# Two cross-attentions on one core: layer-0 values as eight one-head matmuls on 64×32 parts of the array

## The chip, the cores and the metric

The kernel runs on one core of a Trainium2 chip. The metric is device time in microseconds (us), from start to end of one execution; lower is better. A core has a matmul engine (PE, with its weight loads shown apart as PEld), a vector engine (DVE), a scalar engine (ACT), GpSimd (POOL) and a queue engine (SP) that issues most DMAs here. They run side by side and wait for each other by semaphores.

## The reference

Two cross-attention layers follow each other on x, which is 4 batches × 1024 rows × 1024 columns in fp32, with a context of 64 rows a batch. What matters here is the attention of layer 0:

```
q = x Wq + bq;  k = ctx Wk + bk;  v = ctx Wv + bv
# 32 query heads of 32 columns; 8 key/value heads, each shared by 4 query heads
attn = softmax(q k^T / sqrt(32) + mask)      # 64 keys for each row and head
out  = attn v                                # for each head: 64 keys -> 32 columns
x1   = layernorm(out Wo + bo + x)
```

Layer 1 is a second attention with 16 heads of 64 columns and a gated residual. All is computed in fp32.

## The kernel before, in words

The rows of x are worked in 32 tiles of 128 rows (NSUB), eight tiles to a block, two tiles to a pair. The time falls into four stages:

1. Keys and values of both layers are computed from the context (lines 312 to 359). K0 and V0 are kept in one SBUF tile `kv0`, both block-diagonal over two heads: `v0bd` holds, for each batch, head group c and half i, a 128 × 64 matrix whose rows are two heads' 64 keys and whose columns are these heads' 32 columns each, with zeros off the diagonal. `nc.gpsimd.memset(kv0, 0.0)` writes the zeros (line 307) and eight small DMAs the values (line 343).
2. Queries. `query_steps` computes a block's queries by a seven-product scheme (Strassen's, in Winograd's form) on PE (line 551), ACT and DVE add (lines 562, 568), and SP writes them to DRAM as `qTd` (line 565).
3. Attention of layer 0, by `mix(t, count)` for each tile t. The stage interleaves a tile's attention with other work: for tiles 0 to 23 the query steps of the next blocks, for tiles 24 to 31 `folded_queries` (line 832 and 838), which folds layer-1 weights.
4. Output projection of layer 0 (`project`, line 415, with `folded_values`, line 859, among its first pairs), then layer 1. This is some 1215 us and is not touched by the change, but for the form in which it is given Wo.

Within stage 3 a tile goes through these steps. `load_queries` brings q from qTd and the mask (lines 622, 626). `front(c)` makes the scores of half the heads with eight matmuls on 64 rows of the array each (line 655), in pairs that lie on rows 0 to 63 and 64 to 127; DVE adds the mask (line 659), takes the largest (666) and subtracts (669), ACT takes the exponential (673, 681), DVE sums, inverts and divides (686, 687, 690). Then the probabilities have to be turned, keys to partitions: for tiles 0 to 18 (`by_turning`) through DRAM (POOL issues, lines 703 and 707) and two DVE transposes of 32×32 blocks, which the text calls flips (line 391), for tiles 19 to 31 by PE (line 382) and an ACT copy (line 386). Each tile has two turned halves, `pTs[0]` and `pTs[1]`, one for each c.

`values()` then multiplies (line 722). Each of its four matmuls takes 128 rows (two heads' keys) and 64 columns (the same two heads) of the array and 512 moving columns (four query heads × 128 rows of the tile):

```
for c in range(2):
    bank = ps[:, c * 512 : (c + 1) * 512] if by_turning(t) else ps[c]
    for i in range(2):
        nc.tensor.matmul(bank[i * 64 : (i + 1) * 64], v0bd[:, b, c, i, :],
            pTs[c][:, i * 4 : (i + 1) * 4].rearrange("p g l -> p (g l)"), ...)
```

The result lies in two PSUM banks, `big` for tiles 0 to 18 and two `wx` for the others. ACT copies it out (`copy_out`, lines 373 and 375) and writes it to DRAM as `oTd` (line 728), from where the projection loads it. Each fp32 matmul of the program appears in the profile as two weight loads and two matmul records.

A planner, not the order of the source, sets the order of instructions on each engine: it places them by costs that it assumes and by what must be ready. So an edit in one place can move instructions in others. Each engine carries out its own list in order.

Wo comes to `right_weight(wo0, "wa", "wo0")` (line 910) in a row order that the host has set; `block_of` loads each of its four blocks with one DMA of 1 MB (line 148). The buffers of tag `wa` that it goes to are those of the layer-0 query weights, so its loads wait until PE has used these for the last time.

Of the kernel before, what the change touches and what calls it, by code (L numbers as in the profile page):

```python
# [8 lines left out]
F32 = mybir.dt.float32  # L9
# [5 lines left out]
P = 128  # L15
# [4 lines left out]
B = 4  # L20
L = 1024
S = 64
# [7 lines left out]
Q = 32  # L30
NQ = P // Q
QW = H // NQ
PPB = NPAIR // B
HEADS0 = 32
BY_HEAD = 16

# [32 lines left out]
def tile_two_cross_attentions(  # L71
# [25 lines left out]
    nc = tc.nc  # L97

    def sub_ap(t):
        return slice(t * P, (t + 1) * P)  # L100
# [9 lines left out]
    def big():  # L110
        return ps_big.tile([P, 1024], F32, tag="big", name="big")

    def one():
        return big()[:, 0:512]

    def wx():
        return ps_wx.tile([P, 512], F32, tag="wx", name="wx")
# [17 lines left out]
    def new_block(tag, name):  # L135
        return wpool.tile([P, HK, HW], F32, tag=tag, name=name)

    def block_of(w, i, j, tag, name, turned=False):
        t = new_block(tag, name)
        cols = slice(j * HW, (j + 1) * HW)  # L140
        if turned:
            rows = w.rearrange("(a k j) o -> a j k o", a=NQ, j=Q)
            for a in range(NQ):
                nc.sync.dma_start(
                    out=t[a * Q : (a + 1) * Q], in_=rows[a, :, i * HK : (i + 1) * HK, cols]
                )
        else:
            nc.sync.dma_start(
                out=t, in_=w[i * HW : (i + 1) * HW, cols].rearrange("(k p) o -> p k o", p=P)
            )  # L150
        return t
# [28 lines left out]
    def right_weight(w, tag, name, turned=False):  # L180

        r = {"B11": block_of(w, 0, 0, tag, f"{name}_B11", turned)}
        r["T1"] = block_of(w, 0, 1, tag, f"{name}_B12", turned)
        r["B22"] = block_of(w, 1, 1, tag, f"{name}_B22", turned)
        r["B21"] = block_of(w, 1, 0, tag, f"{name}_B21", turned)
        for n in ("T3", "T2", "N4"):
            r[n] = new_block(tag, f"{name}_{n}")
        return r, right_sums(r)
# [7 lines left out]
    kv0pool = open_pool(attention, "kv0", 1, "right")  # L196
# [8 lines left out]
    for i in range(2):  # L205
        t = scratch.tile([P, H], F32, tag="cnat", name=f"ctx_{i}", bufs=2)
# [3 lines left out]
    for w, n in ((wk0, "wk0"), (wv0, "wv0")):  # L210
        t = wpool.tile([P, KC, 256], F32, tag="wb", name=n)
# [91 lines left out]
                )  # L303
        return ct

    kv0 = kv0pool.tile([P, 2048], F32, tag="kv0", name="kv0")
    nc.gpsimd.memset(kv0, 0.0)

    k0bd = kv0[:, 0:1024].rearrange("p (b c n) -> p b c n", b=B, c=2)
    v0bd = kv0[:, 1024:2048].rearrange("p (b c i n) -> p b c i n", b=B, c=2, i=2)  # L310

    ct = transpose_ctx(0)
    for c in range(2):
        ps = one()
# [13 lines left out]
    for bb in range(2):  # L328
        ps = one()
        for k in range(KC):  # L330
            nc.tensor.matmul(
                ps[:, 0:256], ct[:, k, sub_ap(bb)], wkv0[1][:, k, :],
                start=(k == 0), stop=(k == KC - 1),
# [4 lines left out]
    for e in range(2):  # L338
        for i in range(2):
            j = 2 * i + e  # L340
            for c in range(2):
                at = c * P + j * 32
                nc.sync.dma_start(
                    out=v0bd[e * S : (e + 1) * S, :, c, i, e * 32 : (e + 1) * 32],
                    in_=v0d[:, at : at + 32].rearrange("(b s) d -> s b d", b=B),
                )
    ct = transpose_ctx(1)
    kv1 = []
    for w, dst, n in ((w1k, kTd, "k1"), (w1v, vTd, "v1")):
        kvT = kv1pool.tile([P, KC, B * S], F32, tag="k1", name=n)  # L350
        for c in range(KC):
            ps = one() if c % 2 else wx()
            for k in range(KC):
                nc.tensor.matmul(  # L354
                    ps[:, 0:256], w[k // HK, c // HK][:, k % HK, sub_ap(c % HK)], ct[:, k, :],
                    start=(k == 0), stop=(k == KC - 1),
# [256 lines left out]
    def by_turning(t):  # L613


        return t < NSUB - SUB - 5
# [12 lines left out]
    def attend0(t):  # L629
# [12 lines left out]

        n = BY_HEAD if by_turning(t) else 0

# [51 lines left out]
    def outputs0(t):  # L696

        b = t * P // L
        s = probs.pop(t)
        pTs = {}  # L700
        if by_turning(t):

            nc.gpsimd.dma_start(out=p0[t], in_=s)
            pq = pqpool.tile([P, NQ, 512], F32, tag="pq", name=f"pq0_{t}")
            v = p0[t].rearrange("(u i) (a w) -> a i u w", i=Q, a=NQ)
            for a in range(NQ):
                nc.gpsimd.dma_start(out=pq[a * Q : (a + 1) * Q], in_=v[a])

        def flip(c):
            pT = pTs[c] = ppool.tile([P, 8, P], F32, tag="pT", name=f"pT0_{t}_{c}")  # L710
            if by_turning(t):
                turn_quarters(pq, pT, (c * 8, (c + 1) * 8))
                return
            turn(s[:, c * 1024 : (c + 1) * 1024], pT)

        def values():
            oT = opool.tile([P, KC, P], F32, tag="oT", name=f"oT0_{t}")
            ps = big() if by_turning(t) else [wx(), wx()]
            for c in range(2):
                bank = ps[:, c * 512 : (c + 1) * 512] if by_turning(t) else ps[c]  # L720
                for i in range(2):
                    nc.tensor.matmul(  # L722
                        bank[i * 64 : (i + 1) * 64], v0bd[:, b, c, i, :],
                        pTs[c][:, i * 4 : (i + 1) * 4].rearrange("p g l -> p (g l)"),
                        start=True, stop=True,
                    )
            copy_out(oT.rearrange("p g l -> p (g l)"), ps)
            nc.scalar.dma_start(out=oTd[t // 2][:, :, sub_ap(t % 2)], in_=oT)

        return flip, values  # L730

    turned = {}
# [60 lines left out]
    rows, fills = rows0(0)  # L793
# [5 lines left out]
    rows, fills = rows0(1)  # L799
# [88 lines left out]
    def other_work(rows):  # L888

        nonlocal fold, early, bo_sb, w_o, first_outputs  # L890
        for blk in range(1, NBLK):
            steps = query_steps(blk, rows)
            fills = {}
            if blk + 1 < NBLK:
                rows, fills = rows0(blk + 1)
            for n, step in enumerate(steps):
                step()
                if n in fills:
                    fills[n]()
                if n == len(steps) - 1:  # L900
                    load_queries(blk * SUB)
                yield
        queries_cm.close()
        fold = open_pool(fold_cm, "fold", 1)

        early = open_pool(early_cm, "early", 1)
        kT = fold.tile([P, KC, B * S], F32, tag="kvT", name="kT")
        nc.sync.dma_start(out=kT, in_=kTd)
        wch = chunk(wq1, 0, "wq1")
        w_o, w_o_sums = right_weight(wo0, "wa", "wo0")  # L910
        bo_sb = constant(bo0.partition_broadcast(P), [P, H], "bo", F32, fold)
        for k in range(KC):
            ahead = chunk(wq1, k + 1, "wq1") if k + 1 < KC else None
            for step in folded_queries(kT, wch, k):
                step()
                yield
            wch = ahead
            if k == 3:
                run(w_o_sums)
            if k == 5:  # L920
                first_outputs = load_outputs(0)
# [10 lines left out]
    n = 28 * (NBLK - 1) - AHEAD  # L932
# [5 lines left out]
    n = 5 * KC - 2 * AHEAD  # L938
# [59 lines left out]
    for pair in range(NPAIR):  # L998
        r, a = ahead_r, ahead_a
# [29 lines left out]
        if pair == NPAIR - 2:  # L1029
            xq = load_x1(0)  # L1030
            turned = turn_x1(0, xq, o2pool, "o2")
# [79 lines left out]
    for pair in range(NPAIR):  # L1111
# [10 lines left out]
        if (pair + 2) % PPB == 0 and pair + 2 < NPAIR:  # L1122
            b = (pair + 2) // PPB
# [3 lines left out]
        if (pair + 1) % PPB == 0 and pair + 1 < NPAIR:  # L1127
            b = (pair + 1) // PPB
# [68 lines left out]
```

## Time and profile before

| | |
|---|---|
| runs, device time | 1946.58, 1947.51, 1951.64 us; median 1947.51 |
| profiled execution | 1952.53 us, of which the span of its instructions is 1950.5 |
| PE busy, granted clock | 1895.1 us (97%), 0.99 |
| DVE, ACT, POOL busy | 1272.0, 385.2, 289.6 us |
| line 655, matmuls of the scores | 1024 records, 85.7 us |
| line 722, matmuls of the values | 152 records into big, 38.6 us; 104 into wx, 26.1 us |
| flips, pT<-pq, line 391, up to tile 18 | 38, 44.9 us, 1219 ns each |
| stage 3 | from about 194 to 735 us of the span |

A matmul record's own duration holds its way through the array; records overlap, so busy time is the union of them and not their sum. "x8" counts records. `128*64` is the part of the array in use, rows × columns. In the chain of waits a piece lasts until the next piece begins, so there a burst is given by the time that it holds up PE. Windows are stretches of the span; a gap on an engine matters only where the chain passes through it. The median of the runs is 5.0 us below the profiled execution.

### The profile page before, as it was taken

Reading aid. Unit: us, or ns where it says so; the run is one execution under the profiler, and the core shown is the slowest. Engines: PE = TensorE matmul, PEld = TensorE weight load, DVE = VectorE, ACT = ScalarE, POOL = GpSimd, SP = SyncE. Lnnn points to the kernel's source line nnn. Section 1 sums busy time; section 2 is a strip of 40 time slices with the busy share of each in tenths; the row PEclk is TensorE's granted clock in tenths of the full one; section 3 lists DMA queues with packets and bytes.
Section 4 is the critical chain, followed back from the end, with each engine's and each line's share of the span. In section 5 each row is a group of like instructions: output and inputs, shape, how many; then the busy total and the mean of one; then the engine's idle time right before and its main releaser. Section 6 shows DMA issues by size and latency. Waiting matters only on the chain.

```text
span 1950.5 us, 16583 instructions
## 1 busy us (share of the span) xinstructions
PE 1895.1 (97%) x5904; PEld 896.4 (46%) x5904; DVE 1272.0 (65%) x1540; ACT 385.2 (20%) x1028; POOL 289.6 (15%) x198
## 2 busy tenths in 40 slices
PE   8999998998998989999999999999999999999999
PEld 7744444443445654334343444444444444444444
DVE  3424798887878984355367667557665766576653
ACT  1111553643535761221200001000000000000000
POOL 0000111111100104445546542000000000000000
PEclk9999999998999999999999999999999999999999
DMA  8971689796775985666572325374747474747421
GB/s 275 183 190 65 177 237 261 223 254 214 231 214 187 302 258 186 193 217 215 178 231 98 142 83 151 108 172 130 183 119 181 121 183 120 182 125 178 119 87 43
DMA packets 217986, 342.07 MB, mean 175 GB/s; under 512 B 25264, under 2 KB 140336, under 8 KB 212912
## 3 DMA queue, kind: packets, MB, share of 16 engines
q1 hardware_dynamic: 156544, 255.03, 46.4%
q10 hardware_dynamic: 52544, 46.14, 8.6%
q0 software_dynamic: 8816, 39.85, 7.1%
q8 instruction: 46, 0.75, 0.2%
q14 instruction: 36, 0.29, 0.1%
HBM read 203.34 MB, written 137.63 MB: 175 GB/s over the span
## 4 chain that ended last, share of the span: by engine, by line
PE 84%; DVE 9%; DMA 3%; ACT 2%; issue 1%; SPq 0%; DVEq 0%; ACTq 0%
PE wx L415 59%; PE wx L551 14%; PE big L655 3%; DVE s L659 2%; DVE mx L666 2%; PE big L859 1%; PE wx L354 1%; PE big L354 1%; DMA q<-qTd 1%; PE big L722 1%; DVE s L669 1%; DMA qTd<-z 1%; ACT s L673 1%; PE wx L832 1%; DVE sm L686 1%
## 5 line engine op out<-in xcount | busy, mean ns | idle before, releaser
L423 DVE TENSOR_TENSOR r<-wx,r 128x512 f32<-128x512 f32 x224 | 153.5, 686 | 269.0 <-PE wx L415 266.6
L477 ACT ACTIVATE s<-s 128x1024 f32<-128x1024 f32 x32 | 33.7, 1056 | 651.8 <-DVE s L476 642.8
L427 DVE TENSOR_TENSOR s<-wx,key_bias 128x512 f32<-128x512 f32 x64 | 44.1, 689 | 137.3 <-PE wx L415 134.5
L551 PE MATMUL wx<-xT,wq_S 128*128 128x512 f32 x256 | 119.3, 602 | 1.6 <-ACT z L562 1.6
L884 POOL TENSOR_TENSOR r<-r,bo 128x1024 f32<-128x1024 f32 x32 | 79.2, 2482 | 263.1 <-DMA r<-in_x_dram 254.6
L415 PE MATMUL wx<-wo_B,S 128*128 128x512 f32 x256 | 116.8, 599 | 1.4 <-DVE r L423 1.4
L415 PE MATMUL wx<-b_B,pT 128*128 128x512 f32 x256 | 115.8, 593 | 0.6 <-ACT pT L386 0.6
L415 PE MATMUL wx<-b_B,S_p 128*128 128x512 f32 x256 | 116.0, 596 | 0.0
L551 PE MATMUL wx<-xB,wq_A 128*128 128x512 f32 x256 | 115.5, 596 | 0.0
L415 PE MATMUL wx<-a_B,xT 128*128 128x512 f32 x256 | 115.4, 592 | 0.0
L415 PE MATMUL wx<-a_B,S_x 128*128 128x512 f32 x256 | 115.3, 593 | 0.0
L673 ACT ACTIVATE s<-s,mx 128x64 f32<-128x64 f32 x304 | 101.1, 334 | 70.8 <-DVE mx L666 64.6
L415 PE MATMUL wx<-wo_B,o 128*128 128x512 f32 x256 | 113.5, 596 | 0.0
L659 DVE TENSOR_TENSOR s<-big,m 128x1024 f32<-128x1024 f32 x64 | 77.0, 1217 | 46.6 <-PE big L655 46.5
L655 PE MATMUL big<-kv,q 64*128 64x128 f32 x1024 | 85.7, 298 | 15.0 <-DMA q<-qTd 14.9
L655 PEld LDWEIGHTS big<-kv,q 64*128 64x128 f32 x1024 | 73.2, 200 | 51.2 <-issue 45.2
L966 POOL TENSOR_TENSOR r<-r,gamma 128x1024 f32<-128x1024 f32 x32 | 76.0, 2376 | 137.1 <-DVE r L284 137.1
L967 POOL TENSOR_TENSOR r<-r,beta 128x1024 f32<-128x1024 f32 x32 | 80.4, 2513 | 2.4
L415 PEld LDWEIGHTS wx<-wo_B,S 128*128 128x128 f32 x256 | 47.3, 190 | 67.1 <-issue 53.6
L391 DVE STREAM_TRANSPOSE pT<-pq 128x1024 f32<-128x1024 f32 x66 | 77.9, 1218 | 0.0
L690 DVE TENSOR_TENSOR s<-s,sm 128x1024 f32<-128x1024 f32 x64 | 77.2, 1222 | 1.0
L415 PEld LDWEIGHTS wx<-wo_B,o 128*128 128x128 f32 x256 | 48.0, 190 | 63.5 <-issue 63.0
(159 smaller groups left out, 2993.6 us busy)
## 6 DMA issues: line engine op xcount, KB each, us to landing
p<-s POOLq DMA_DIRECT2D x19, 1024.0 KB, 8.3
pq<-p POOLq DMA_DIRECT2D x76, 256.0 KB, 6.2
xq<-in_x_dram SPq DMA_DIRECT2D x64, 256.0 KB, 10.2
q<-qTd SPq DMA_DIRECT2D x32, 512.0 KB, 8.3
oTd<-oT ACTq DMA_DIRECT2D x32, 512.0 KB, 7.4
ad<-a SPq DMA_DIRECT2D x16, 1024.0 KB, 7.3
o<-oTd SPq DMA_DIRECT2D x16, 1024.0 KB, 8.8
r<-in_x_dram SPq DMA_DIRECT2D x32, 512.0 KB, 4.1
```

The lines of the kernel that those rows point to most:

```text
L391: nc.vector.transpose(dst.rearrange("p k (u i) -> p k u i", i=Q), t[:, :, k0 * Q : k1 * Q].rearrange("p u (k j) -> p k u j", j=Q),)
L415: nc.tensor.matmul(bank, a[s][:, k, :], w[m][:, k, :], start=first and k == 0, stop=last and k == HK - 1, skip_group_check=True,)
L423: nc.vector.tensor_tensor(at, bank, at, ALU.add)
L427: nc.vector.tensor_tensor(at, bank.rearrange("p (h s) -> p h s", s=S), bias.unsqueeze(1).to_broadcast([P, 512 // S, S]), ALU.add,)
L551: nc.tensor.matmul(bank, w_q[a][:, k, sub_ap(i)], rows[b][:, k, :], start=first and k == 0, stop=last and k == HK - 1, skip_group_check=True,)
L655: nc.tensor.matmul(ps[:, at : at + P], q[on, c * 4 + g, :], k0bd[on, b, c, :], start=True, stop=True,)
L659: nc.vector.tensor_tensor(quarters[:, :, c * 8 : (c + 1) * 8], ps.rearrange("p (k a l) -> p a k l", a=NQ, l=Q), mask.rearrange("p e (h l) ...
L673: nc.scalar.activation(heads[:, 0, k], heads[:, 0, k], AF.Exp, bias=mx[:, 0, k : k + 1], accum_out=sm[:, 0, k : k + 1],)
L690: nc.vector.tensor_tensor(heads[:, e], heads[:, e], wide(sm[:, e]), ALU.mult)
L884: nc.gpsimd.tensor_tensor(ru, ru, bo_sb, ALU.add)
L966: nc.gpsimd.tensor_tensor(r[u], r[u], gamma0_sb, ALU.mult)
L967: nc.gpsimd.tensor_tensor(r[u], r[u], beta0_sb, ALU.add)
```

## The change

V0 is kept as it is, without zeros: `v0` holds for each batch, c and i the 64 keys × 32 columns of one head on partitions 0 to 63 (e = 0) and of another on 64 to 127 (e = 1). `values()` makes eight matmuls instead of four. Each has one head's 64 keys on one row half of the array (rows e·64) and 32 of its columns (columns (2c + i)·32), with 512 moving columns as before. The eight parts cover the array once. The bank is now chosen by e, not by c, so the two row halves write to different banks.

With that the rows of `oT` lie in another order, and Wo has to match: `block_of` gets a third form, `"heads"`, which loads each of the four blocks with four DMAs of 32 partitions (256 KB each). `kv0` becomes a quarter smaller, and the memset covers the keys' half alone.

```diff
-        if turned:
+        if turned == "heads":
+            rows = w.rearrange("(c g i e d) o -> c i e d g o", c=2, g=4, i=2, e=2)
+            for a in range(NQ):
+                nc.sync.dma_start(
+                    out=t[a * Q : (a + 1) * Q], in_=rows[a // 2, a % 2, i][:, :, cols]
+                )
+        elif turned:
...
-    kv0 = kv0pool.tile([P, 2048], F32, tag="kv0", name="kv0")
-    nc.gpsimd.memset(kv0, 0.0)
+    kv0 = kv0pool.tile([P, 1536], F32, tag="kv0", name="kv0")
+    nc.gpsimd.memset(kv0[:, 0:1024], 0.0)
...
-    v0bd = kv0[:, 1024:2048].rearrange("p (b c i n) -> p b c i n", b=B, c=2, i=2)
+    v0 = kv0[:, 1024:1536].rearrange("p (b c i d) -> p b c i d", b=B, c=2, i=2)
...
-                    out=v0bd[e * S : (e + 1) * S, :, c, i, e * 32 : (e + 1) * 32],
+                    out=v0[e * S : (e + 1) * S, :, c, i, :],
...
             for c in range(2):
-                bank = ps[:, c * 512 : (c + 1) * 512] if by_turning(t) else ps[c]
                 for i in range(2):
-                    nc.tensor.matmul(
-                        bank[i * 64 : (i + 1) * 64], v0bd[:, b, c, i, :],
-                        pTs[c][:, i * 4 : (i + 1) * 4].rearrange("p g l -> p (g l)"),
-                        start=True, stop=True,
-                    )
+                    for e in range(2):
+                        bank = ps[:, e * 512 : (e + 1) * 512] if by_turning(t) else ps[e]
+                        on, at = slice(e * S, (e + 1) * S), (2 * c + i) * 32
+                        nc.tensor.matmul(
+                            bank[at : at + 32], v0[on, b, c, i, :],
+                            pTs[c][on, i * 4 : (i + 1) * 4].rearrange("p g l -> p (g l)"),
+                            start=True, stop=True, tile_position=(e * S, at),
+                        )
...
-        w_o, w_o_sums = right_weight(wo0, "wa", "wo0")
+        w_o, w_o_sums = right_weight(wo0, "wa", "wo0", "heads")
```

## The prediction

> **What bounds the kernel now.** I read first the sums by engine, to see who is nearly full; then the windows, cut where the chain of waits changes hands, because the change lives in one stage; then the chain and the order of time inside them, for what a shorter burst is worth there.
>
> ```profile
> PE 1895.1 (97%) x5904; PEld 896.4 (46%) x5904; DVE 1272.0 (65%) x1540; ACT 385.2 (20%) x1028; POOL 289.6 (15%) x198
> ```
>
> ```profile
> 194.00:244.00 50.00, 50.00 (x216) 23.75 (x216) 36.69 (x38) 25.43 (x108) 6.21 (x11) 1.00 0.62 174
> 244.00:334.00 90.00, 83.76 (x326) 37.15 (x326) 80.52 (x79) 42.52 (x180) 13.69 (x25) 0.99 0.91 242
> 334.00:411.00 77.00, 76.95 (x320) 37.08 (x318) 67.06 (x69) 41.49 (x178) 11.06 (x21) 0.97 0.82 239
> 411.00:480.00 69.00, 61.34 (x232) 26.93 (x230) 54.22 (x52) 28.18 (x111) 10.86 (x20) 0.97 0.83 243
> 480.00:567.00 87.00, 85.99 (x366) 41.11 (x366) 70.15 (x70) 38.24 (x123) 10.41 (x19) 0.97 0.73 215
> 567.00:735.00 168.00, 150.66 (x1019) 98.84 (x1016) 144.35 (x145) 102.11 (x154) 6.15 (x3) 0.95 0.79 247
> ```
>
> The columns are length, then busy time of PE, PEld, DVE, ACT and POOL, clock and DMA. The reader is to see two kinds of stretch. In 194–244, 334–411 and 480–567 PE has hardly a gap, and the chain of waits is all PE. In the other three PE has 6, 8 and 17 us of gaps, DVE is 89, 79 and 86% busy, and the chain runs along DVE and, twice, through the write and reload of qTd. All values matmuls (line 722) lie in these six. Two bursts on the chain, one whole and one that the built order has split, and from the timeline one burst that waits and the flips it waits for:
>
> ```profile
> 376.52 1.87 PE big L722 x8
> 378.39 1.09 PE big L655 x16
> ...
> 393.74 1.02 PE big L722 x4
> 394.76 0.42 PE big L655 x2
> 395.17 1.01 PE big L722 x4
> ```
>
> ```profile
> 319.79 2.12 PE L722 MATMUL big<-pT,kv 128*64 128x512 f32 x8 [0.65 <-DVE pT L391]
> ```
>
> ```profile
> 318.40 2.36 DVE L391 STREAM_TRANSPOSE pT<-pq 128x1024 f32<-128x1024 f32 x2
> ```
>
> Each program matmul is two records. A whole burst (8 records, four matmuls) holds PE 1.87 us. The records of the trace show why: they start in pairs, 0.006 us apart, at 0, 0.48, 0.91 and 1.34 us; so the two 64-column halves already stream together, and a pair takes 0.43 us as a full-width record does. 4 × 0.43 = 1.72, and 0.15 for change of layout and a first weight load. The last two lines show the other limit: the two flips of one tile end 1.13 us apart, and the burst began right after the first.
>
> **What the Trainium skill says.** "TensorE: Matmul & The Clock Gate", Part 3: matmuls on different row and column strips run at once, starting about 4 ns apart; sixteen tiles of 32×32 at 512 columns came out 10.6 times faster. The trace agrees for two column halves (above) and for two row halves (line 655: pairs 0.007 us apart, sixteen records in 1.09 us); eight parts it does not show. "TensorEngine Tiling (Array Packing)", Restrictions and Gotchas: row tiles must not share a PSUM bank at one time, which the change respects by giving each row half a bank. The first page, Part 1, on the clock gate: an idle window of about 3.4 us halves the clock. Here half-clock windows last 3.4, 6.8 or 10.2 us and stand behind PE's longest gaps (at 329, 473, 614 us).
>
> **The change part by part.**
>
> *Burst alone.* Eight matmuls, each on its own 64×32 part: all first passes side by side, then all second passes. 0.48 + 0.43 + 0.09 for the exit = 1.00 us (the split half above, two matmuls on two parts, takes just that: 1.01), plus 6 × 0.007 = 0.04 for the further starts. I take 1.02 against 1.87: 0.85 us, times 32 = 27 us at most.
>
> *What holds it back: the second flip.* The four matmuls of c = 1 need the second pT. Before, its lateness hid behind the 0.86 us of c = 0. Now all want to start together, and a second flip that is d late costs d. Set the end of each flip against the first start of its burst, in the records: in 8 of the 32 tiles d is 0.89 to 1.0 us (PE was waiting for the first flip, and the second comes 1.13 later), in 5 more, all turned on PE, 0.86 to 2.2; in the rest −1.07 to 0.58. A burst with d near 1 costs 1.03 + 1.01 = 2.04 whether it has four matmuls or eight: saved, nothing.
>
> *What stands on the path.* Saving = 1.87 − (1.02 + max(0, d + 0.05)), bursts on the chain only. Tile 0 (d 0.20): 0.6. 334–411: tile 6 (d −0.08) 0.85; tile 7 (0.89) 0; tile 8 (0.43) 0.4; tile 9 (0.98), split, 2.45 with 0.11 of score work inside becomes 2.04: 0.3; half of tile 10: 0.15; sum 1.7. 480–567: tile 14 (−0.67) 0.85, tile 15 (0.45) 0.35, tiles 16 and 17 (0.23) 0.57 each, tile 18, split, 0.5; sum 2.8. 567–735: tile 26 0.7, tile 23 (0.86) 0. The last tile: before, c = 1 stands behind a matmul of line 859 that waits for vT (landed at 727); in the built order after, all eight come first and four matmuls of line 415 stand ahead of line 859. Values end at 724.66 + 1.17 + 1.01 = 726.8 instead of 729.2, less 0.5 for the line-859 pair now done later: 1.8. Total 7.6 us.
>
> *Order.* The built order moves: it split 10 bursts before and splits 2 after; values of tiles 9 to 21 stand two to six matmuls earlier, and DVE's flips with them, often ahead of a division. Each such place is worth up to a few us to either side; I take 0 and keep ±4 for the range.
>
> *Wo.* Its four loads become sixteen, with 2 KB pieces as before. Twelve more issues on SP at about 0.4 us (0.38 to 0.43 in the trace) are 5 us of SP's time around 520–570, in front of q and mask loads. Those go out a tile (about 15 us) ahead, and Wo is first used for its sums near 598: hidden. Without that cover: up to 5 us late for a score matmul; kept in the ±4. Queueing behind a busy weight buffer is no new wait (SP waits on PE for line 148 14.2 us in three places already).
>
> *Nothing.* The memset halves, 1.81 to about 0.9 us on POOL; behind it the identity is ready at 3.0, and PE waits for ctx until 4.64. The eight V0 loads keep number and size. copy_out reads as many columns.
>
> **Sum.** The profiled execution took 1952.53, span 1950.5 and 2.0 around it; 7.6 off gives 1944.9. The median of the runs is 5.0 lower, so 1947.5 − 7.6 = 1939.9.
>
> **The rivals.**
>
> 1. *The gain is swallowed* (0.25). DVE is 87% busy in 334–411; once PE arrives earlier it waits for the first flip in more tiles, each then has d near 1, and the qTd reload (9.8 us at 470) takes the rest; one more half-clock window of 6.8 us costs 3.4. Against it: tiles 14 to 17 had their first flip 0.7 to 1.8 us before PE came. Gain −4 to 5: 1942 to 1951.
>
> 2. *The full stretches are not the only ones* (0.15). In 244–334 PE is 93% busy as well, and DVE waits for score matmuls 46.5 us in all (20 times). If DVE gets its scores earlier everywhere, the other tiles' 0.4 to 0.86 count too: all 32 by the formula give some 14, and with merged bursts 15 to 22: 1926 to 1932.
>
> 3. *Slower: four column parts over the same 64 rows don't stream together* (0.08). Place: the burst. If only a row pair runs at once, eight matmuls take 4 × 0.86 + 0.15 = 3.6 us, 1.7 more than now; on some 15 bursts of the chain +26, on all 32 +55: 1973 to 2002. It decides at four wide: then a burst takes 1.87 and nothing is lost. The two-wide overlap both ways speaks against it.
>
> 4. *The change doesn't do what it says*: parts run four wide, burst unchanged at 1.87; inside rival 1's numbers.
>
> **How the numbers follow.** 0.3% is 5.8 us, about what a measurement of this kernel can tell from no change. The likeliest case (0.52) spans gains of 3 to 14, and most of it lies over 5.8: 0.43 faster, 0.09 same. Rival 1: 0.19 same, 0.05 slower, little faster. Rival 2 is faster, rival 3 slower. Together 0.59 faster, 0.28 same, 0.13 slower. The likeliest case alone would span 1933 to 1945. For 8 in 10 I reach to 1928, which takes most of rival 2, and to 1951, which takes rival 1; rival 3 stays out.
>
> **What would show it right or wrong.** Right: a values burst of 16 records with eight starts within 0.06 us and 1.0 us on the chain where the flips are early, about 2.0 where they are not; matmul time of the line (38.6 and 26.1 us now, in its two groups) down by 14 to 27 us, while PE's gaps before it that DVE or ACT ends (7.1 and 6.3 us now) grow; line 415's first matmul some 2 us earlier after the last tile; the stretch after 735 unchanged at about 1215. Wrong: bursts of 1.9 or 3.6 us (the overlap), a span that falls by 15 or more (slack on DVE was larger than I read), or a longer wait at q or mask loads near 560–620 (SP).

## The result, and the profile after

The changed kernel takes 1946.39 us (median of 12 runs) beside 1949.38 for the kernel before on the same chip: ratio 0.9979, 95% interval 0.9968 to 0.9989, or some 4 us less. (The ratio is the one on record; the two medians themselves lie 3.0 us apart.) The forecast was 7.6 us less. A burst costs what the prediction's formula says, but most of the 4 us comes with the new order of instructions, and by the profiles more than half of that at the last tile. The shorter bursts themselves bring about 1 us, which can't be told from nothing, where the sum had 5.8 for them and for the joining of split ones.

| | before | after |
|---|---|---|
| profiled execution, span | 1952.53, 1950.5 | 1946.74, 1944.5 |
| values matmuls busy, two groups | 38.6 + 26.1 | 33.9 + 19.9 |
| first matmul of the projection to the end | 1221.3 | 1221.8 |
| half-clock time, mean of the runs | 34 to 37 (five sets of runs) | 45 |

Half-clock time is the time that the granted clock of PE stood at half, worked out as 2 × (1 − mean granted clock) × span. Lines move down in the new file: the scores are line 662, the values 733, the flips 398, the projection 422, the subtraction of the largest 676, the fold of the layer-1 weights 843.

The sums by engine and the windows, columns as before:

```profile
PE 1885.5 (97%) x6160; PEld 892.9 (46%) x6160; DVE 1276.9 (66%) x1540; ACT 384.7 (20%) x1028; POOL 288.4 (15%) x198
```

```profile
194.00:244.00 50.00, 50.00 (x234) 24.43 (x234) 36.98 (x39) 25.84 (x108) 6.21 (x11) 1.00 0.61 179
244.00:334.00 90.00, 85.48 (x387) 38.10 (x386) 84.00 (x83) 42.74 (x181) 13.69 (x25) 0.98 0.92 258
334.00:411.00 77.00, 76.17 (x369) 34.59 (x368) 69.01 (x71) 42.61 (x183) 13.66 (x25) 1.00 0.83 234
411.00:480.00 69.00, 63.44 (x285) 29.22 (x283) 57.78 (x56) 33.01 (x140) 10.40 (x19) 0.98 0.82 245
480.00:567.00 87.00, 85.32 (x428) 39.46 (x428) 69.87 (x76) 36.38 (x96) 8.23 (x15) 1.00 0.81 221
567.00:735.00 168.00, 144.08 (x1049) 97.95 (x1046) 136.96 (x134) 100.19 (x155) 7.07 (x3) 0.90 0.78 241
```

The full stretches are still full, but the same 735 us end with less: the work of the last window ends earlier in it, and its clock is 0.90 where it was 0.95. PE's busy time there fell by 6.6 us, in part because the stage ended earlier. The clock is the first thing to be noticed that no term of the sum allows for.

The bursts, from the chain of waits (start, length until the next piece):

```profile
232.99 1.25 PE big L733 x16
...
353.80 2.10 PE big L733 x16
...
371.35 1.48 PE big L733 x16
...
509.78 2.10 PE big L733 x16
...
528.29 1.21 PE big L733 x16
```

These are tiles 0, 7, 8, 16 and 17. Before, tile 16 took 1.87:

```profile
525.43 1.87 PE big L722 x8
```

Two from the timeline, one with both flips early and one that waits:

```profile
250.67 1.09 PE L733 MATMUL big<-pT,kv 64*32 64x512 f32 x16
251.69 1.16 PE L662 MATMUL big<-kv,q 64*128 64x128 f32 x16
```

```profile
264.92 2.10 PE L733 MATMUL big<-pT,kv 64*32 64x512 f32 x16 [0.28 <-DVE pT L398]
266.95 1.16 PE L662 MATMUL big<-kv,q 64*128 64x128 f32 x16
```

In the first the eight starts lie within 0.046 us, the second passes begin at 0.453, and the scores start 1.02 us after the burst's start. In the second the four matmuls of c = 1 start at 1.034, and the burst holds PE 2.03. The bursts between are those whose second flip is somewhat late. So eight parts stream side by side. The groups of the line over stage 3 (busy, mean ns | idle before, and who ended it) say the same:

```profile
L733 PE MATMUL big<-pT,kv 64*32 64x512 f32 x304 | 33.9, 617 | 6.2 <-DVE pT L398 6.2
L733 PE MATMUL wx<-pT,kv 64*32 64x512 f32 x208 | 19.9, 611 | 2.9 <-ACT pT L393 2.8
```

Busy time is down by 10.9 us, short of the 14 to 27 that the prediction gave, while the gaps that a flip or a copy ends grew from 1.9 and 2.0 us to 6.2 and 2.9 (the same groups of the kernel before, cut to stage 3 as here). Taken as in the prediction, with the weight loads' waits, they grew from 6.3 to 16.3 us behind flips and from 7.1 to 9.5 behind copies.

### The profile page after: what moved, and what is told of

Read it like the earlier page. It is cut to its first block, busy times and chain, and to the rows that moved or that the text cites. A ratio compares the mean times of both kernels' runs of the same rounds, so it can differ in the third digit from the quotient of the medians.

```text
span 1944.5 us, 17115 instructions
## 1 busy us (share of the span) xinstructions
PE 1885.5 (97%) x6160; PEld 892.9 (46%) x6160; DVE 1276.9 (66%) x1540; ACT 384.7 (20%) x1028; POOL 288.4 (15%) x198
## 4 chain that ended last, share of the span: by engine, by line
PE 81%; DVE 11%; DMA 3%; issue 2%; ACT 2%; SPq 0%; POOL 0%; DVEq 0%; ACTq 0%
PE wx L422 59%; PE wx L558 12%; PE big L662 2%; DVE mx L673 2%; DVE s L666 2%; PE wx L361 1%; PE big L361 1%; PE big L870 1%; DVE s L676 1%; DVE sm L693 1%; DMA q<-qTd 1%; DVE pT L398 1%; DMA pq<-p 1%; DVE s L697 1%; PE wx L843 1%
## 5 line engine op out<-in xcount | busy, mean ns | idle before, releaser
L434 DVE TENSOR_TENSOR s<-wx,key_bias 128x512 f32<-128x512 f32 x64 | 44.2, 690 | 137.2 <-PE wx L422 137.2
```

What stands on the lines that cost most here:

```text
L434: nc.vector.tensor_tensor(at, bank.rearrange("p (h s) -> p h s", s=S), bias.unsqueeze(1).to_broadcast([P, 512 // S, S]), ALU.add,)
```

## The experiments

Each kernel was timed against the kernel before, on the same chip. 0.001 is 1.95 us. Where two kernels are compared through their ratios, the ± is worked out from the half widths of both intervals, as the root of the sum of squares. "Pinned" means that every engine's list of instructions is kept in a given order, by dependencies in the program that cost no wait. The leads in tables come from one profile each, so the medians judge, and the leads tell where to look: the kernel before itself differs from profile to profile. In the one of `f4_joined` below, which has the old form and but for six bursts the old order, the values of tile 6 start 6.6 us earlier than in the profile of before, with no half-clock window ahead of them. The changed kernel pinned and otherwise left alone was not run; the kernel before, pinned with one small edit, comes within 1 us of itself in f4, `e4_wo_parts` and `h3_before_adds`.

### Order and bursts apart

`e1_old_order` is the new form pinned to the order of the kernel before. `e2_new_order` is the old form pinned to the order of the changed kernel.

```diff
+ # e1: after.py,  every engine's list as in before.py
+ # e2: before.py, every engine's list as in after.py
+ tc.add_manual_dep(by_name[next], this, NoSync)   # for each pair of neighbours
```

> The changed kernel with every engine's list pinned to the order of the kernel before: each old values matmul is replaced in its place by its two, each Wo load by its four. Nothing else differs from the changed kernel. Theory A (the bursts themselves make the gain; what the tile stage saves is partly given back in the last eight tiles to half-clock windows and waits): 2 to 7 us faster than the kernel before; bursts of 1.0 us where the flips are early, in the ten split places two half bursts of 1.0 us each as before. Rival B (the planner's new order makes the gain, the bursts only move waits): within 2 us of the kernel before. Rival C (the new order costs time in the last eight tiles, where the tile stage was 16 us ahead and the end only 6): 8 to 14 us faster than the kernel before.

> The kernel before, four values matmuls of 128 rows and 64 columns, with every engine's list pinned to the order of the changed kernel (each pair of new matmuls replaced by its old one; for tiles 19 and 20, which the new order splits, the four stand together, since the old form can't be split there). Theory A: the old bursts stand earlier against the flips and hold PE 1.87 to 2.04 us, so within 3 us of the kernel before, or a few us slower. Rival B: 3 to 6 us faster than the kernel before, with the short bursts adding nothing. Rival C: 3 to 8 us slower than the kernel before, the loss lying after tile 22.

Measured: e1 0.9994 (0.9985 to 1.0002), half-clock time 42 us; e2 0.9983 (0.9974 to 0.9992), half-clock time 34 us. So **the order alone brings 3.3 us** (1.6 to 5.1), and the bursts alone 1.2, which can't be told from nothing. On the new order the bursts add 0.8 ± 2.7 us (0.9979 against 0.9983).

A good part of the order's gain lies at the last tile. There the chain is, before and then after:

```profile
727.10 1.09 PE big L859 x2
728.19 1.01 PE wx L722 x4
729.20 3.63 PE wx L415 x8
```

```profile
722.76 3.63 PE wx L422 x8
726.39 1.92 PE big L870 x8
```

Before, the second half of the values stands behind a matmul of line 859 that waits for a DMA; in the new order that line (870 in the new file) comes after the projection's first matmuls. From the start of the last tile's values to the projection's first matmul it takes 4.47 us before, 2.43 in e2, 3.98 in e1 and 2.17 after, so at most 0.5 of it goes with the bursts. From the same start to the end of the span it takes 1225.2 to 1226.4 us in four profiles with the old bursts and the old order (before, f4, e4, h3) and 1222.7 to 1224.0 in four with the new order (e2, after, f3, h1): some 2 us.

`f4_joined` keeps the old form and order and joins the six split bursts of tiles 2, 3, 9, 10, 12 and 18; `e4_wo_parts` keeps all and brings Wo in sixteen loads.

```diff
# f4, list of PE, tile 9:   V V  S  V V   ->   V V V V  S      (V values, S scores)
# e4, block_of, one of four loads of a block:
-                nc.sync.dma_start(out=t, in_=rows)
+                for a in range(NQ):
+                    nc.sync.dma_start(out=t[a * Q : (a + 1) * Q], in_=rows[a])
```

> The kernel before in its own order but for one thing: of tiles 2, 3, 9, 10, 12 and 18, whose four values matmuls the planner had split by one or two other matmuls, the four now stand together and the others follow. It asks what in the new order made the old bursts 3 us faster. If the splits: each costs 2.45 us against 2.04 with 0.1 to 0.9 of other work inside, 0.3 us each, so 1 to 3 us under the kernel before (ratio 0.9985 to 0.9995). If the places of flips, divisions and loads: within 1 us of the kernel before.

> The kernel before in its own order (pinned), with one part of the change alone: Wo's four loads become sixteen of 32 partitions each, in the row order of before. As predicted: within 2 us of the kernel before. Rival E (sixteen issues on SP delay the q and mask loads behind them, which is what the changed kernel lost between tiles 18 and 24): 2 to 6 us slower, with scores of tiles 21 to 24 starting later than in the kernel before.

Measured: f4 0.9995 (0.9982 to 1.0009), e4 0.9995 (0.9982 to 1.0009). Wo's extra loads cost nothing that the interval of ±2.6 us shows, and joining bursts gains nothing that it shows. Apart from the last tile, which of the order's many moves bring what is left wasn't tried.

### Late tiles: the values made more than once

The profile of after runs ahead of before by 15.7 us at the values of tile 21, and by 4.1 at tile 31. Over the same stretch e2 loses 4.7 of 6.5 us, 3.4 of them at tiles 21 to 23: there the new order pays for work that it had put off (up to tile 21 it has made 8 records less of the query products, some 0.43 us each, and by tile 22 it has made them). After itself loses a further 2.4 us from tile 22 to 23, where PE waits 4.56 us for the reload of qTd and before waits 2.95. From tile 23 on after loses 5.5 and e2 1.3. The first thought was that short bursts leave PE idle in the late tiles and that its clock falls. So the values of tiles 23 to 31 were made twice or three times there, the same result written again, which is more work for nothing.

```diff
-            for c in range(2):
+            for c in [0, 1] * (2 if t >= 23 else 1):     # e3, f1; 3 in f2
```

> The changed kernel in its own order (pinned), but tiles 23 to 31 make their eight values matmuls twice, the second set writing the same numbers over the first. PE gets 9 times about 0.9 us more to do, in the stage that came out longer. Theory A, clock part (shorter bursts leave PE idle long enough that the clock is halved; 34 us of half-clock windows after tile 22 against 17 before): the windows fall to 10 to 25 us and the time is the same or up to 5 us below the changed kernel, although PE does 8 us more. Rival D (PE is on the path there and the windows follow from other waits): 4 to 8 us above the changed kernel, windows still about 34 us.

> The run with the new bursts in the order of before, now with the values of tiles 23 to 31 made twice (the second set writes the same numbers). The clock theory, from the granted clocks of the runs: half-clock time was 35 us in the kernel before, 42 in the run with the new bursts in the old order, 45 in the changed kernel, and 33.5 where tiles 23 to 31 made their values twice; and within each kernel a run's time rises by about 0.35 us for each us of half clock. So here half-clock time falls to 33 to 36 us and the ratio to 0.9970 to 0.9985 (3 to 6 us under the kernel before), 2 to 4 us below the single set in the same order. Rival (the doubled set only happened to suit the new order): half-clock time may fall, but the ratio stays at 0.999 to 1.001.

> The changed kernel in its own order, with the values of tiles 23 to 31 made three times. Clock theory: half-clock time falls no further or little (30 to 34 us) while each burst holds PE 0.9 us more, so 0 to 5 us above the run with two sets, still at or below the changed kernel. Rival (any delay of PE in these tiles helps, by shifting it against DVE and ACT): another 2 to 4 us below the run with two sets.

Measured: e3 (the changed kernel's order) 0.9962 (0.9949 to 0.9975), half-clock time 34 us; f1 (the order of before) 0.9987 (0.9976 to 0.9997), 31 us; f2 0.9973 (0.9964 to 0.9982), 31 us. Nine further bursts make the kernel 3.3 ± 3.3 us faster than the changed one, which is just at the edge of the noise; a third time brings nothing more (f2 lies 2.1 ± 3.1 above e3). In the order of before they bring 1.4 ± 2.6 (f1 against e1), less than expected and not told from nothing.

`f3_tiles_twice` was to finish the table with long bursts in tiles 0 to 22 and short ones later.

```diff
+            for c in ([0, 1] if t >= 23 else [0, 0, 1, 1]):
```

> The changed kernel in its own order, with the values of tiles 0 to 22 made twice in the order c = 0, 0, 1, 1, so that their bursts hold PE about 1.9 us and hide the second flip as the old ones did; tiles 23 to 31 keep the short burst. With the runs so far this completes a table of old or new burst in the early and in the late tiles, all in the new order. Theory: short bursts are worth 4 to 8 us in the early tiles and cost 3 in the late ones, so this run, long early and short late, is the slowest of the four: ratio 0.999 to 1.002, half-clock time 40 us or more. Rival (short bursts are worth nothing anywhere, the order gives it all): ratio 0.997 to 0.9985.

It came to 0.9998 (0.999 to 1.0007), with 32 us of half-clock time where over 40 was expected: a miss. Its bursts don't stand for the old ones, since with a late flip they hold PE 2.9 us instead of 2.0, so it decides nothing.

### A filler that waits for nothing

A burst made twice also waits for its flips. `g1_fold_warm` has instead one extra matmul, the identity times kv0, into the bank that the values then overwrite. `h4_oldburst_warm` puts the same into the old bursts, in the changed kernel's order.

```diff
+            if t >= 23:
+                nc.tensor.matmul(ps[0], ident, kv0[:, 0:512], start=True, stop=True)
             for c in range(2):
```

> The changed kernel in its own order, but ahead of the values of tiles 23 to 31 one extra matmul of the identity, whose result is overwritten (two records, 0.86 us of TensorE, needing no flip). Theory A (short late bursts leave TensorE idle enough that its clock is halved more often; any filling of the late tiles repairs it): half-clock time 31 to 36 us instead of 45, ratio to before 0.996 to 0.9975, as with the values made twice. Rival B (what helped in the doubled kernel was when the doubled burst ends against the flips of its own tile, not TensorE being busy): half-clock time stays 42 to 48 and the ratio 0.9975 to 0.9985, that of the changed kernel, or higher by the 9 x 0.86 us.

> The old bursts (block-diagonal V) in the order of the changed kernel, with one extra identity matmul ahead of the values of tiles 23 to 31. The same order without the extra matmul came out at 0.9983, with 34 us of half-clock time. If the filler repairs what short bursts opened: no gain here, 0.998 to 0.9995. If a filler helps the late tiles whatever the burst: 0.9955 to 0.997, half-clock time 20 to 28 us.

Measured: g1 0.9946 (0.9932 to 0.996), half-clock time 31 us: 6.4 ± 3.4 us faster than the changed kernel, with nine matmuls more, which is more than theory A asked for. h4 0.9973 (0.9959 to 0.9986), 26 us: 2.0 ± 3.2 better than e2, between the two values expected. Between g1 and h4 the burst differs and what goes with its form: **with the late tiles filled, the short bursts are worth 5.3 ± 3.8 us**. That the filler does more for short bursts than for old ones is likely but not shown: 6.4 less 2.0 is 4.5 ± 4.7. Groups of after, then of g1, over 604 to 735 us:

```profile
L843 PE MATMUL wx<-kT,wq1T 64*128 64x256 f32 x224 | 44.2, 440 | 7.8 <-ACT a L849 5.6 <-ACT wq1T L380 1.7 <-ACT oT L380 0.5
...
L662 PE MATMUL big<-kv,q 64*128 64x128 f32 x256 | 30.0, 338 | 4.6 <-DMA q<-qTd 4.6
```

```profile
L845 PE MATMUL wx<-kT,wq1T 64*128 64x256 f32 x224 | 38.7, 402 | 5.2 <-ACT a L851 4.1 <-ACT wq1T L380 1.1
...
L662 PE MATMUL big<-kv,q 64*128 64x128 f32 x256 | 26.0, 310 | 3.6 <-DMA q<-qTd 3.6
```

The same count of the same matmuls is 9.5 us shorter in these two groups, since fewer of them fall into half-clock windows: outside the windows the mean of one is 394 and 392 ns in line 843 and 845, and 279 in line 662 in both, while inside it is some 650 and 433. The windows of these profiles from about 604 to 735 us sum to 34 us after, 20 in g1, and 17 in before (from 612).

The same filler was put in front of the first scores of tiles 8, 16 and 24, where PE waits for the reload of qTd (4.70, 7.23 and 2.95 us in before, not the 8 to 10 that g3's expectation has): `g4_before_warm` in the kernel before, `g3_twice_warm` in the changed kernel with late values made twice.

```diff
+            for _ in range({8: 5, 16: 5, 24: 3}.get(t, 0) if c == 0 else 0):
+                nc.tensor.matmul(ps[:, 0:512], ident, kv0[:, 0:512], start=True, stop=True)
             for g in range(4):
```

> The changed kernel with the values of tiles 23 to 31 made twice, and 5, 5 and 3 extra matmuls of the identity (0.86 us each, overwritten) ahead of the first scores of tiles 8, 16 and 24, where TensorE waits 8 to 10 us for the reload of qTd. Theory A (half-clock time costs, some 0.3 to 0.5 us per us): half-clock time falls from 33 to 15 to 26 us and the ratio from 0.996 to 0.993 to 0.9955. Rival B (half-clock time goes with slow steps but does not make them slow; or the fillers end after the reload and cost what they hold): half-clock time may fall, the ratio stays 0.9955 to 0.998.

> The kernel before in its own order, with only the 5, 5 and 3 extra matmuls of the identity ahead of the first scores of tiles 8, 16 and 24. Theory A: half-clock time from 34 to 18 to 27 us, ratio 0.996 to 0.999. Rival B: ratio 0.9995 to 1.002.

Measured: g3 0.9963 (0.9952 to 0.9973), half-clock time 23 us; g4 1.0003 (0.9992 to 1.0015), 26 us. Ten us less of half-clock time and no gain: the clock alone failed as a reason. In g3 the five fillers held PE 4.4 us at tile 8, where after waited only 0.9. In g4 they fit the wait at tile 8:

```profile
327.96 4.45 PE L652 MATMUL big<-kv,ident 128*128 128x512 f32 x10
332.35 1.83 PE L656 MATMUL big<-kv,q 64*128 64x128 f32 x28
```

Here before had a gap of 4.70 us ahead of its scores. g4 was 4.1 us ahead at tile 24, yet only 0.6 at tile 27. Something between was not clock.

### What sat between: two adds of GpSimd

GpSimd adds the bias bo to r, the rows of x that the projection's first two tiles will need. Timeline of g4, DVE and then POOL:

```profile
640.93 3.11 DVE L691 TENSOR_TENSOR s<-s,sm 128x1024 f32<-128x1024 f32 x1
...
648.60 4.51 DVE L670 TENSOR_TENSOR s<-s,mx 128x1024 f32<-128x1024 f32 x2
```

```profile
639.93 3.02 POOL L885 TENSOR_TENSOR r<-r,bo 128x1024 f32<-128x1024 f32 x1 [97.93 <-ACT oT L374]
649.50 2.53 POOL L885 TENSOR_TENSOR r<-r,bo 128x1024 f32<-128x1024 f32 x1 [6.54 <-DMA r<-in_x_dram]
```

A DVE operation that takes 1.22 us elsewhere takes 3.11 beside an add of r and bo on GpSimd, and one of a pair 3.38. In the changed kernel:

```profile
628.45 2.34 DVE L673 TENSOR_REDUCE mx<-s 128x16 f32<-128x1024 f32 x2
...
629.86 2.37 POOL L895 TENSOR_TENSOR r<-r,bo 128x1024 f32<-128x1024 f32 x1 [99.02 <-DMA oTd<-oT]
630.71 3.73 DVE L676 TENSOR_TENSOR s<-s,mx 128x1024 f32<-128x1024 f32 x2
```

The largest (673, one tensor in) runs through beside the add. The subtraction (676, two tensors in) starts at 630.71 and takes 2.60 us for the first of its two; it ends 1.1 us after the add does, as if it had begun only then. The Trainium skill, "GPSIMD Engine Reference", Specifications, names contention of GpSimd with VectorE instructions that have two SBUF inputs. The trace agrees, 2.60 us against 1.22. In before the adds ran at 641.49 and 652.35; no DVE operation beside them took over 1.30 us, and the second add took 3.13 us instead of 2.35 itself. The meeting is no property of the new form: f4, in the old one, has a subtraction of 3.37 us beside an add, and h4 one of 3.39. The chain of after goes through the slowed operation, and what follows it, until PE begins again:

```profile
630.79 2.53 DVE s L676
...
633.35 1.06 ACT s L688
...
634.94 1.12 PE wx L389 x4
```

PE sat idle for 2.83 us there and its clock was halved from 634.8 on, for 6.8 us. So a lead that brings the adds onto another operation can pay twice. The second add of after met nothing that it slowed. The adds need nothing but bo and their loads, so they run at no fixed point of a tile. To take the meeting out of the late tiles, SP issues the two loads of r behind the last loads of tile 31; the adds then run at 718 to 724 us in h1, 715 to 721 in h2 and 728 to 734 in h3. They meet VectorE there as well: in h1 two operations of the projection (lines 408 and 409) take 2.01 and 2.72 us, which in after take 0.69. So what h1 shows is the gain net of that.

```diff
# list of SP
-  o2 load, r load 0, ..., r load 1, ..., loads of tiles 25 to 31
+  o2 load, ..., loads of tiles 25 to 31, r load 0, r load 1
```

> The changed kernel in its own order, except that SyncE issues the loads of r for the first two row blocks behind the last loads of tile 31, so that the two GpSimd adds that wait for them come after the tiles. Theory B (the adds slow VectorE in the late tiles): no VectorE operation of a late tile over 1.9 us, 1 to 3 us faster than the changed kernel, ratio to before 0.9963 to 0.9975. Theory A (half clock on late matmuls): half-clock time stays near 45 us and the ratio near 0.998 (0.9975 to 0.9985).

> The changed kernel with one extra identity matmul ahead of the values of tiles 23 to 31, and with the loads of r moved as in the run before. If both causes are there and add up: 0.993 to 0.9942. If the filler had only moved the adds to a harmless place: as the kernel with the filler alone, 0.9945.

> The kernel before in its own order with the loads of r moved in the same way. Its profile showed no VectorE operation slowed by the adds in the late tiles. Theory B as a cause of what the change lost: within 0.0005 of 1. If the adds cost before as often as after: 0.9985 to 0.9993, and they explain no difference.

Measured: h1, the changed kernel so, 0.9956 (0.9944 to 0.9968), half-clock time 39 us, 4.5 ± 3.1 us faster than the changed kernel, more than theory B gave. h2, with g1's filler too, 0.9935 (0.9924 to 0.9947), half-clock time 25 us, 2.1 ± 3.5 below g1. h3, the kernel before so, 0.9996 (0.9987 to 1.0005): nothing there that can be told from noise. h2 against h1 is the cleanest test of the filler, since no add runs in the late tiles of either: **4.1 ± 3.2 us, with 14 us less of half-clock time**. Moving the adds alone had already shortened the two groups that g1 shortened. In h1:

```profile
L843 PE MATMUL wx<-kT,wq1T 64*128 64x256 f32 x224 | 39.6, 409 | 8.1 <-ACT a L849 5.5 <-ACT wq1T L380 1.7 <-ACT oT L380 0.9
...
L662 PE MATMUL big<-kv,q 64*128 64x128 f32 x256 | 27.8, 326 | 4.3 <-DMA q<-qTd 4.3
```

They took 44.2 and 30.0 us in after, so not all of g1's 9.5 us there is the filler's. The DVE line of h1 over the late tiles (min/median/max ns), where after had a maximum of 2599:

```profile
L676 DVE TENSOR_TENSOR s<-s,mx x16: 1212/1217/1221, 614.5 to 706.9; 128x1024 f32<-128x1024 f32 x16
```

Lead over the profile of before at the start of a tile's values, in us:

| tile | e2 | after | h1 | g1 | h2 |
|---|---|---|---|---|---|
| 5 | 2.4 | 3.0 | 1.9 | 3.4 | 2.9 |
| 13 | 6.4 | 11.2 | 9.8 | 12.4 | 11.0 |
| 21 | 6.5 | 15.7 | 14.6 | 16.7 | 14.9 |
| 23 | 3.1 | 9.6 | 8.8 | 11.6 | 9.4 |
| 25 | 3.2 | 4.5 | 8.9 | 10.7 | 8.5 |
| 31 | 1.8 | 4.1 | 7.7 | 8.9 | 10.1 |

Up to tile 23 the four new kernels are alike within 3 us. Of these the changed kernel alone loses 5.1 us in the two tiles with its meeting; e3, whose profile has the same meeting, loses 5.2 there. In g1 an add meets line 676 as well (2.47 us, at 639), and g1 loses 0.9 us from tile 25 to 27.

Three last kernels: `h5_old_adds` is e1 with the loads of r moved, `h7_before_warm_adds` is g4 with them moved, and `h6_all` has the change, g1's filler, fillers ahead of tiles 16 (5) and 24 (4), and the loads moved.

```diff
# h6, on top of h2
+            for _ in range({16: 5, 24: 4}.get(t, 0) if c == 0 else 0):
+                nc.tensor.matmul(ps[:, 0:512], ident, kv0[:, 0:512], start=True, stop=True)
```

> The new bursts in the order of the kernel before (which alone came to 0.9994), with the loads of r behind tile 31's loads, so that the two GpSimd adds come after the tiles. Theory B (the adds ate the bursts' gain in the late tiles): 0.996 to 0.9978, no VectorE operation of a late tile over 1.9 us. Theory A (half clock alone, opened by short bursts): 0.9985 to 1.0. The kernel before with the same move came to 0.9996.

> The kernel before with the 5, 5 and 3 identity matmuls ahead of the first scores of tiles 8, 16 and 24 (1.0003 alone) and with the loads of r moved (0.9996 alone). If the fillers save time at the stalls and the adds ate it: 0.9965 to 0.9985. If half-clock windows at the stalls cost nothing: 0.9992 to 1.0008.

> The changed kernel with one identity matmul ahead of the values of tiles 23 to 31, the loads of r moved, and 5 and 4 identity matmuls ahead of the first scores of tiles 16 and 24, where TensorE waits 4 to 5 us for qTd. If half-clock windows after these stalls lie on the path: 0.991 to 0.993, half-clock time 10 to 18 us. If they do not, or the fillers overrun the stalls: 0.9935 to 0.995.

Measured: h5 0.9984 (0.9975 to 0.9994), half-clock time 42 us; h7 0.9982 (0.9971 to 0.9992), 22 us; h6 0.9922 (0.9909 to 0.9936), 20 us, in the first of its two ranges for the ratio. h7 is 4.1 ± 3.0 us better than g4, as if the adds had eaten what the fillers won at the stalls. Its profile doesn't show where, since the lead still falls from 3.1 us at tile 23 to 0.2 at tile 31. h5 is a miss for the adds as the whole reason: 2.0 ± 2.5 us better than e1, at the edge of what theory A gave. In the old order the loss from tile 23 to 31 is the same with and without the adds, 3.7 us in both profiles. This loss says little, though: against the same profile of before, kernels with the old bursts and the old order lose 1.3 (h3), 1.7 (f4), 2.8 (e4) and 3.9 us (g4) over these tiles. h6 is the fastest kernel of the study, some 15 us below before, though not told apart from h2 (2.5 ± 3.5).

## Why the prediction was right or wrong

**The burst: right.** Eight parts at once, 1.02 us with early flips and 2.03 with a second flip 1.03 late. Rivals 3 and 4 fell. Given the lateness d that the new profile has, the formula gives each burst of tiles 0 to 18 within some 0.03 us. The exception is tile 5, which falls into a half-clock window and holds PE 2.90.

**"Bursts on the chain only": the step that failed.** The sum took each d from the profile of before, as if PE would come to the burst no earlier against the flips. It did come earlier, and waited:

| tile | d before | d after | formula with d before | measured after | measured e1 |
|---|---|---|---|---|---|
| 6 | −0.08 | 0.88 | 1.02 | 1.93 | 2.03 |
| 7 | 0.89 | 0.98 | 1.96 | 2.03 | 2.03 |
| 8 | 0.43 | 0.43 | 1.50 | 1.48 | 1.48 |
| 14 | −0.67 | 0.41 | 1.02 | 1.46 | 1.02 |
| 15 | 0.45 | 0.98 | 1.52 | 2.03 | 1.92 |
| 16 | 0.24 | 0.98 | 1.31 | 2.03 | 1.28 |
| 17 | 0.23 | 0.16 | 1.30 | 1.21 | 1.28 |

These are the bursts of the sum that were whole before. It had 3.6 us for them; they hold PE 1.0 us less after, and 2.1 in e1. Elsewhere d fell (tile 9, from 0.98 to −0.02), which the sum didn't have either. The gaps before the line show the same (6.2 us from 1.9 after, 4.3 in e1). This is the first half of rival 1. In the time of the whole kernel, e1 keeps the old order and so could show only part of the 7.6: without the joined bursts and the last tile some 4.9 was left, of which 1.2 ± 1.7 us came. A burst that shortens on the chain as it was drawn shortens the time only until the next wait.

**The last tile: right in kind.** Its values' start to line 422's first matmul took 4.5 us before and 2.2 after: 2.3 against 1.8 predicted. It is a gain of the order, as the prediction said. **Wo, the memset and the stage after: right** as far as the runs can tell (e4; 1221.3 and 1221.8 us).

**"Order: I take 0": not settled.** e2 measures the whole order at 3.3 ± 1.8 us, but some 2 of it is the last tile, which the sum had as an item of its own, and another part can be the joined bursts. What is left for the places that were set to 0 is about 1 us, which can't be told from nothing. That about half of the 7.6 us came is owed more to the last tile and the new order than to the bursts that the sum was made of.

**The late tiles: a loss that the sum didn't have.** It had 0.7 us for 567 to 735 and no loss. After tile 23 after loses 5.5 us, where kernels with the old bursts and the old order lose 1.3 to 3.9 against the same profile. Two edits win time back there. First, a filler for PE's idle time: 6.4 ± 3.4 us alone, 4.1 ± 3.2 with the adds away. Rival 1 had the cause as "one more half-clock window of 6.8 us costs 3.4"; half-clock time rose by some 7 us in the old order (e1) and 12 in the new (45 against e2's 34). The Trainium skill tells of the pattern, "TensorE: Matmul & The Clock Gate", HAM oscillation: a stage of short bursts with waits between them is throttled again and again. The trace agrees in kind: the six late windows of after begin inside a PE gap, or within 1.4 us of its end. But the page's waits last over 3.4 us, and here only one of the six gaps does (4.6 us); the others last 1.6 to 2.8. Second, the two adds on GpSimd, of which one meets VectorE: moving them wins 4.5 ± 3.1 us in the changed kernel, 2.1 ± 3.5 with the filler in, nothing clear of noise in before (h3). The prediction listed no POOL work in stage 3 but the turning, and had no step for a lead that moves DVE against an engine with a clock of its own. The two overlap: both edits together bring 8.6 ± 3.0 us (h2), less than 6.4 + 4.5. Both are shown for the changed kernel alone; in the old order neither (1.4 ± 2.6 and 2.0 ± 2.5) can be told from nothing.

**Rival 1** named the right outcome, a gain of −4 to 5, with half of the reasons: the first flips and a half-clock window, but not the adds. **Rival 2** is not what happened, but with the late tiles filled and the adds moved the changed kernel reaches 12.7 us below before (h2), near its figure of 14, of which 3.3 are the order's.

Open: how often the meeting happens in runs other than the profiled ones; whether a filler helps by the clock alone or also by when it lets the values start, since no run delays PE without giving it work; and how much of the order's gain lies outside the last tile. Half-clock time is no price by itself: in g4 and g3 it fell by 10 us without a gain. Moving the loads of r also takes them out of SP's way in tiles 24 and 25; h3 bounds what this gives in before, not in the changed kernel.

## What to carry to other kernels

Shortening an engine's bursts on the chain pays only up to the next operand: don't take an operand's lateness from the old profile, because the engine will come earlier. In this kernel the idle time that opened went with half-clock windows over work that is on the chain; after such a change compare the mean duration of untouched matmuls in each stage, not only that of the edited line. When a change shifts one stage in time by some us, look for free-running operations of GpSimd that may now meet two-input VectorE operations, and try their loads at another place, where a slowed VectorE holds nothing up. Time a change in the old order and the old form in the new order before you credit the edit.

## What the hardware showed beyond expectation

- Adding useless work made the changed kernel faster: nine matmuls more, 6.4 ± 3.4 us less, and 4.1 ± 3.2 with the adds out of the way. With fillers at the stalls as well it came to 15 us below before.
- A GpSimd add of 128×1024 (2.35 us) that began first held a two-input DVE operation up to 3.4 instead of 1.22 us; where DVE had begun first, the add took 2.8 to 3.5 (e2, before, e1). A DVE reduce beside it was not slowed (1.21), nor was an add of the mask, which has one of its two inputs in PSUM (1.23 in after, at 639.87).
- Eight fp32 matmuls on 64×32 parts start about 7 ns apart, their second passes at 0.453 us, and hold PE 1.02 us; with the second operand 1.03 us late they hold it 2.03, no less than four on 128×64 parts (2.04).
